# A selective-scan layer on one NeuronCore: when the next chunk's softplus, norm and gate projections are issued

## The chip, the cores and the metric

The kernel runs on one core of a Trainium2 chip. A core has five engines that run their own instruction queues in order and wait for each other through semaphores: TensorE (PE, matrix products into PSUM banks), VectorE (DVE), ScalarE (ACT, elementwise functions), GpSimd (POOL) and SyncE (SP, which issues most DMAs here). The metric is the device time of one execution in microseconds; the time before is the median of three runs.

## The reference, cut to what matters

The network has four layers; the change lies in the last one, a state-space layer, run here on an input of 3 images, 256 channels and 48 x 48 = 2304 tokens. `x` is the input of the layer after a group norm.

```python
mu = jnp.mean(xf, axis=-1, keepdims=True)
var = jnp.mean(jnp.square(xf - mu), axis=-1, keepdims=True)
xn = (xf - mu) * jax.lax.rsqrt(var + 1e-05) * norm_w + norm_b
xz = jnp.einsum('blc,dc->bld', xn, in_proj_w)
x_in, z = jnp.split(xz, 2, axis=-1)
...
xc = xc + conv_b[None, :, None]
u = jax.nn.silu(xc).transpose(0, 2, 1)
x_dbl = jnp.einsum('bld,ed->ble', u, x_proj_w)
...
dt = jax.nn.softplus(jnp.einsum('blr,dr->bld', dt_raw, dt_proj_w) + dt_proj_b)
A = -jnp.exp(A_log)

def step(hst, inp):
    dt_t, B_t, C_t, u_t = inp
    dA = jnp.exp(dt_t[:, :, None] * A)
    hst = hst * dA + dt_t[:, :, None] * B_t[:, None, :] * u_t[:, :, None]
    y_t = jnp.einsum('bdn,bn->bd', hst, C_t)
    return (hst, y_t)
...
y = ys.transpose(1, 0, 2) + u * D_param
y = y * jax.nn.silu(z)
out = jnp.einsum('bld,cd->blc', y, out_proj_w)
```

There are 512 inner channels and 16 states for each, so 8192 recurrences, each over 2304 tokens, for each of 3 images.

## The kernel before, in words

**Chunks and steps.** The layer runs over 18 chunks of 384 tokens (3 images, 6 chunks each). The scan of a chunk is eight steps (m = 0 to 3, one block of 128 inner channels each, times h = 0, 1, half of the states), and a step is eight scans over 384 tokens. A half step is four scans; the schedule counts half steps from 0 to 15 in a chunk, so half steps 8 to 11 are the fifth and sixth step, 12 to 15 the seventh and eighth. Below, "scan (11, 3)" is the last (counted from 0) of the four scans of half step 11.

**A scan and its decay.** Scan on DVE (L1785) takes a decay factor exp(dt A) that ACT has written to one of three PSUM slots (L1777). Right after issuing scan n the program issues decay n+3, which needs the slot that scan n frees. So the decay issued behind scan (j, p) is the one that scan (j, p+3) needs, three scans on (behind (13, 0) for (13, 3), behind (14, 0) for (14, 3)); ACT can be ahead of DVE by that much and no more. Between steps DVE also fills part of the next step's state tile (L1738; 2 instructions where the next step begins a block (h = 0), 1 where it does not) and, at the end of each h = 1 step, multiplies y with the gate (L1826). POOL fills the rest of the state tile (L1752) and, when all eight scans of a step are done, multiplies the states with C (L1802); PE then sums them (L1819).

**What runs beside the scan.** Everything else of the layer is prepared for later chunks while the scan of the current one runs: x norm two chunks ahead, projections, convolution taps, u, B, C, dt and the gate z one chunk ahead, the output projection one chunk behind. Lists (`plan`, `after`, `gating`, `last_of_all`) hand each stage a half step and a place in it: BEGIN, MID, DONE and LATE are behind the first, second, third and fourth scan and its decay, and PE_ is the end of the half step (behind the step's fills and its POOL product where the half step closes a step). Within one place, the order is that of the lists. `keep_order` holds PE, DVE, ACT and POOL to the order of issue, so a stage that waits for another engine holds up everything behind it on its own queue, the decays on ACT's among them.

**Two banks for all products.** All the preparing products use the same two PSUM banks, `bank[0]` and `bank[1]` (tiles `ps_g`). A product cannot start until the stage that reads the bank before it is done, and the ACT or DVE stage behind it cannot start until the product is.

**Stages on the path of the change** (names as in the code): `project_dt` (two products of 17 rows, L1317) gives dt for two of four blocks into both banks; `softplus` takes their absolute value (two ACT instructions, L1326), Exp of minus that (L1327) and Ln of one plus that (L1328); `take_dt` (four DVE instructions, L1333 and L1334) adds the positive part and makes dt times u; `keep_dt` (two ACT copies, L1338) empties the banks and sends dt and dt u to DRAM by two DMAs on SP. The second pair of blocks repeats all that. `group_scale` (two ACT, L1212), `less_mean` (four products, eight recorded instructions, L1221), `centre` (two copies, L1234, and a Square, L1236), `square_mean` (L1228), `inverse_root` (Ln and Exp on the bank, L1240 and L1241), `normalise` (one DVE product, L1245) and `tokens` (a short copy and two ACT, L1253 and L1255) are the norm. `project_z` and `take_z` (L1348, L1356) make z in four parts. `project_x`, `take_x`, `taps`, `take_u` (L1262, L1268, L1272, L1280) make u. The Silu of z and of u (L1285) sit between two loads of ACT's function tables.

## Time and profile before

| | us |
|---|---|
| median of 3 runs | 3430.42 (3429.17 to 3431.03) |
| profiled execution | 3427.89 |
| its span | 3426.0 |
| first scan of the layer starts at | 2019.0 |
| last scan starts at | 3403.1 |
| DVE, busy in the span | 2929.3 |
| ACT | 2379.0 |
| POOL | 1430.1 |

The scan layer is the last 1407 us of the span. A row of the profile's groups names the line, the engine, the operation, the output and inputs by tile, the count, the busy time with the mean of one, and the idle time of the engine just before these instructions with what ended it. The timeline gives start and length of each instruction or run of equal ones, in us from the start of the span, and in brackets the idle time before it and who ended it. Lengths are those that can be seen: a scan shows 0.93 us, and back to back they start every 0.85 us. The tables of stretches give the busy time of each engine in each stretch and the clock that TensorE was granted (PEclk, 1.00 is full speed).

### The profile page before, as it was taken

The page shows a single profiled execution, that of the slowest core. Times are in us where ns is not written, and L with a number is a line of the kernel's source. Part 1 is how long each engine was busy: PE and PEld are TensorE (multiplying, and loading weights), DVE is VectorE, ACT ScalarE, POOL GpSimd, SP SyncE. Part 2 cuts the span into 40 slices and gives each one's busy share as a digit, 9 for nine tenths or more (in the row PEclk, how much of TensorE's full clock was granted, in tenths as well). Part 3 has the DMA queues.
Part 4 walks back from the last instruction along what each step waited for, and adds up shares of the span by engine and source line. Part 5 has one row for each costly group of instructions (what it writes and reads, how often), then busy time and mean ns, then how long its engine had stood idle before and what let it go on. Part 6 is the DMA issues. An engine that isn't in the chain of part 4 may idle for free. (4 is left out here: it accounts for less than half of the span.)

```text
span 3426.0 us, 51520 instructions
## 1 busy us (share of the span) xinstructions
PE 3057.3 (89%) x19882; PEld 1446.1 (42%) x19882; DVE 2929.3 (86%) x3302; ACT 2379.0 (69%) x3596; POOL 1430.1 (42%) x385
## 2 busy tenths in 40 slices
PE   7999999999999999879999978788888888787885
PEld 4334343453333435447777743333333333333331
DVE  3799899959999896479965369999999999999997
ACT  2688888848888885432224458888788888888874
POOL 0000000000000000210000049999999999999997
PEclk9999999999999999989999998888898898888986
DMA  4000000010000002746501134545444444454441
GB/s 167 27 8 10 8 8 7 11 42 5 10 8 8 7 8 90 243 165 222 186 22 51 42 98 102 117 106 125 107 121 103 115 105 116 105 119 123 111 116 43
DMA packets 167170, 272.89 MB, mean 80 GB/s; under 512 B 30129, under 2 KB 134641, under 8 KB 164994
## 3 DMA queue, kind: packets, MB, share of 16 engines
q1 hardware_dynamic: 153682, 249.44, 26.8%
q10 hardware_dynamic: 13232, 20.06, 1.8%
q8 instruction: 158, 2.59, 0.3%
q14 instruction: 98, 0.80, 0.1%
HBM read 222.08 MB, written 47.10 MB: 79 GB/s over the span
## 5 line engine op out<-in xcount | busy, mean ns | idle before, releaser
L642 ACT ACTIVATE pt<-ps_s 128x1024 f32<-128x1024 f32 x972 | 942.3, 1022 | 154.8 <-PE ps_s L638 142.1
L1785 DVE TENSOR_TENSOR_SCAN hs<-ps_da,hs 128x385 f32<-128x385 f32 x1152 | 1005.4, 936 | 37.3 <-ACT ps_da L1777 34.3
L857 DVE TENSOR_TENSOR part<-part,pt 128x2048 f32<-128x2048 f32 x396 | 906.6, 2289 | 41.2 <-ACT pt L642 18.5
L1777 ACT ACTIVATE ps_da<-dtr,u 128x384 f32<-128x384 f32 x1152 | 657.6, 582 | 225.3 <-DVE hs L1785 214.3
L164 POOL TENSOR_TENSOR rstd<-ve,mhalf 128x2 f32<-128x2 f32 (+1 forms) x26 | 16.3, 629 | 1477.2 <-DVE ve L162 1477.2
L638 PE MATMUL ps_s<-q,kt 32*128 32x512 f32 (+1 forms) x4320 | 576.4, 592 | 0.1
L651 PE MATMUL acc<-pt,vt 128*32 128x512 f32 (+1 forms) x4320 | 520.9, 561 | 0.2
L1532 PE MATMUL ps_c<-vt,u 128*128 128x288 f32 x1728 | 431.3, 410 | 21.9 <-DVE u L263 21.9
L1802 POOL TENSOR_TENSOR hc<-hs,x 128x3072 f32<-128x3072 f32 x72 | 445.4, 6186 | 9.5 <-DVE hs L1785 7.5
L1802 POOL TENSOR_TENSOR hc<-hs,bc 128x3072 f32<-128x3072 f32 x71 | 437.7, 6165 | 8.0 <-DVE hs L1785 6.4
L1532 PEld LDWEIGHTS ps_c<-vt,u 128*128 128x128 f32 x1728 | 330.3, 192 | 118.0 <-issue 20.9
L638 PEld LDWEIGHTS ps_s<-q,kt 32*128 32x128 f32 x4320 | 195.3, 183 | 199.1 <-issue 120.2
L1819 PE MATMUL ps_y<-hc,u 128*32 128x384 f32 x2304 | 254.2, 566 | 18.9 <-POOL hc L1802 18.5
L1752 POOL TENSOR_TENSOR hs<-dtur,x 128x1536 f32<-128x1536 f32 x72 | 248.2, 3448 | 7.2 <-DMA dtur<-dtud 7.2
L1752 POOL TENSOR_TENSOR hs<-dtur,bc 128x1536 f32<-128x1536 f32 x72 | 248.8, 3456 | 0.0
L651 PEld LDWEIGHTS acc<-pt,vt 128*32 128x32 f32 x4320 | 94.4, 108 | 353.4 <-issue 326.7
L1272 PE MATMUL ps_g<-u 128*128 128x384 f32 x576 | 200.7, 497 | 21.5 <-ACT u L1268 21.4
L1317 PE MATMUL ps_g<-wconv,u 17*128 17x384 f32 x144 | 79.2, 684 | 105.2 <-ACT x L1338 79.6
L1272 PEld LDWEIGHTS ps_g<-u 128*128 128x128 f32 x576 | 107.5, 191 | 111.7 <-ACT u L1268 42.7
L1221 PE MATMUL ps_g<-wconv,u 128*128 128x384 f32 x144 | 85.7, 767 | 63.8 <-ACT x L1338 63.3
L1819 PEld LDWEIGHTS ps_y<-hc,u 128*32 128x32 f32 x2304 | 65.5, 119 | 180.7 <-issue 141.5
L322 POOL MEMSET xpad<- 128x212 f32 x12 | 5.7, 471 | 307.3 <-ACT xpad L1583 227.5
(249 smaller groups left out, 3825.1 us busy)
## 6 DMA issues: line engine op xcount, KB each, us to landing
wconv<-in_we SPq DMA_DIRECT2D x144, 384.0 KB, 4.2
dtr<-dtd SPq DMA_DIRECT2D x288, 192.0 KB, 3.7
dtur<-dtud SPq DMA_DIRECT2D x288, 96.0 KB, 4.1
wconv<-xd SPq DMA_DIRECT2D x36, 384.0 KB, 4.7
x<-bcd SPq DMA_DIRECT2D x72, 192.0 KB, 5.5
dtd<-x SPq DMA_DIRECT2D x36, 384.0 KB, 4.6
bc<-bcd SPq DMA_DIRECT2D x72, 192.0 KB, 5.0
yc<-ycat ACTq DMA_DIRECT2D x18, 576.0 KB, 4.7
```

Source lines behind the costliest of these rows:

```text
L638: nc.tensor.matmul(s[:, j, cols], kt[r, mt * P : (mt + 1) * P], q[r, :n], start=True, stop=True,)
L642: nc.scalar.activation(p[:, h0 : h0 + 2, :], s, AF.Exp)
L651: nc.tensor.matmul(acc[h * HD : (h + 1) * HD, :n], vt[:, mt, g * P + h * HD : g * P + (h + 1) * HD], p[:, h, cols], start=mt == 0, stop=mt ...
L857: ): nc.vector.tensor_tensor(part, first, p, ALU.add)
L1221: nc.tensor.matmul(bank[to], w3v["less"][:, int(to != ct), :], k.xg[:, ct, :], start=ct == 0, stop=ct == CT - 1,)
L1272: nc.tensor.matmul(bank[m % 2], w3v["taps"][:, m, tap, :], w3v["xi"][:, m % 3, tap : tap + CH], start=tap == 0, stop=tap == DCONV - 1,)
L1532: nc.tensor.matmul(pc[:, :HN], u[:, i, dy, ct, m * P : (m + 1) * P], vt[:, i, ct, dy * TW : dy * TW + HN], start=ct == 0 and dy == 0, stop ...
L1752: nc.gpsimd.tensor_tensor(states(s)[:, :, 2:4, 1:], chunks[at].rows[m][1].unsqueeze(1).broadcast_to([P, 2, 2, CH]), b_rows(s, 0, 2), ALU.mult,
L1777: nc.scalar.activation(slots[n % 3][:, 1 : CH + 1], chunks[at].rows[m][0][:, q, :], AF.Exp, scale=amat[:, col : col + 1],)
L1785: nc.vector.tensor_tensor_scan(b, slots[(8 * s + part) % 3][:, : CH + 1], b, 0.0, ALU.mult, ALU.add)
L1802: nc.gpsimd.tensor_tensor(hc, tiles[s][:, :, :, 1:], cb.broadcast_to([P, 2, 4, CH]), ALU.mult)
L1819: nc.tensor.matmul(k.y_ps[32 * q : 32 * q + 32, :CH], fold, hc[:, g, q, :], start=False, stop=h == 1 and g == 1,)
```

## The change

`softplus` becomes three stages (`take_abs`, `exp_of`, `log_of`), and the Square leaves `centre` for a stage of its own (`squares`). The plan's places move: softplus of the first pair goes from behind (9, LATE) to (9, MID), (9, DONE) and (9, LATE); its `take_dt` two places up, its `keep_dt` two, and `project_dt` of the second pair from the end of half step 10 to its second place. The second pair's softplus is taken apart over (10, LATE), (11, BEGIN) and (11, MID), with `take_dt` at (11, LATE) and `keep_dt` at (12, BEGIN). The norm moves up by two to four scans, from `group_scale` to `tokens`. The four parts of z are all made and taken within half steps 13 to 15, where before the last two were taken in half step 0 of the next chunk. `take_x` and `taps` of the third block move from (3, LATE) to (3, DONE). Each engine runs the same instructions as before, in another order. The code that runs ahead of the first scan calls the parts in the old order.

```diff
     def centre(k):
         for ct in range(CT):
             nc.scalar.copy(k.xg[:, ct, :], bank[ct])
+
+    def squares(k):
         k.sq = room(k, "sq")
         nc.scalar.activation(k.sq, k.xg, AF.Square)
...
-    def softplus(k, m0):
-
-        both = k.dt[:, m0 : m0 + 2, :]
+    def take_abs(k, m0):
         for j in range(2):
             nc.scalar.activation(k.dt[:, m0 + j, :], bank[j], AF.Abs)
+
+    def exp_of(k, m0):
+        both = k.dt[:, m0 : m0 + 2, :]
         nc.scalar.activation(both, both, AF.Exp, scale=-1.0)
+
+    def log_of(k, m0):
+        both = k.dt[:, m0 : m0 + 2, :]
         nc.scalar.activation(both, both, AF.Ln, bias=1.0)
...
     plan = [
-        (12, MID, 2, group_scale),
-        (12, PE_, 2, less_mean),
-        (13, LATE, 2, centre),
-        (13, PE_, 2, square_mean),
-        (14, MID, 2, inverse_root),
-        (15, MID, 2, normalise),
-        (15, LATE, 2, tokens),
...
-        (3, LATE, 1, lambda k: take_x(k, 2)),
-        (3, LATE, 1, lambda k: taps(k, 2)),
+        (3, DONE, 1, lambda k: take_x(k, 2)),
+        (3, DONE, 1, lambda k: taps(k, 2)),
...
-        (9, LATE, 1, lambda k: softplus(k, 0)),
-        (10, DONE, 1, lambda k: take_dt(k, 0)),
-        (10, LATE, 1, lambda k: keep_dt(k, 0)),
-        (10, PE_, 1, lambda k: project_dt(k, 2)),
-        (11, LATE, 1, lambda k: softplus(k, 2)),
-        (12, MID, 1, lambda k: take_dt(k, 2)),
-        (12, DONE, 1, lambda k: keep_dt(k, 2)),
+        (9, MID, 1, lambda k: take_abs(k, 0)),
+        (9, DONE, 1, lambda k: exp_of(k, 0)),
+        (9, LATE, 1, lambda k: log_of(k, 0)),
+        (10, BEGIN, 1, lambda k: take_dt(k, 0)),
+        (10, MID, 1, lambda k: keep_dt(k, 0)),
+        (10, MID, 1, lambda k: project_dt(k, 2)),
+        (10, LATE, 1, lambda k: take_abs(k, 2)),
+        (11, BEGIN, 1, lambda k: exp_of(k, 2)),
+        (11, MID, 1, lambda k: log_of(k, 2)),
+        (11, LATE, 1, lambda k: take_dt(k, 2)),
+        (12, BEGIN, 1, lambda k: keep_dt(k, 2)),
+        (11, DONE, 2, group_scale),
+        (12, BEGIN, 2, less_mean),
+        (12, LATE, 2, centre),
+        (13, BEGIN, 2, squares),
+        (13, BEGIN, 2, square_mean),
+        (13, LATE, 2, inverse_root),
+        (14, MID, 2, normalise),
+        (14, LATE, 2, tokens),
     ]
 
     after = [
-        (0, MID, 0, lambda k: k.at and take_z(k, 2, 0)),
-        (0, MID, 0, lambda k: k.at and take_z(k, 3, 1)),
...
     gating = [
-        (13, PE_, 1, lambda k: project_z(k, 0, 0)),
-        (14, DONE, 1, lambda k: take_z(k, 0, 0)),
-        (14, PE_, 1, lambda k: project_z(k, 1, 0)),
-        (15, MID, 1, lambda k: take_z(k, 1, 0)),
-        (15, PE_, 1, lambda k: project_z(k, 2, 0)),
-        (15, PE_, 1, lambda k: project_z(k, 3, 1)),
+        (13, BEGIN, 1, lambda k: project_z(k, 0, 0)),
+        (13, PE_, 1, lambda k: project_z(k, 1, 0)),
+        (13, LATE, 1, lambda k: take_z(k, 0, 0)),
+        (14, DONE, 1, lambda k: take_z(k, 1, 0)),
+        (14, DONE, 1, lambda k: project_z(k, 2, 0)),
+        (14, PE_, 1, lambda k: project_z(k, 3, 1)),
+        (15, MID, 1, lambda k: take_z(k, 2, 0)),
+        (15, DONE, 1, lambda k: take_z(k, 3, 1)),
     ]
```

More of the change, by code (lines that the diff above doesn't have):

```diff
@@ L1458, in early_preparation @@
         centre(k)
+        squares(k)
         tap_matrices(0)
@@ L1491, in early_preparation @@
             stage(k)
+            if stage is centre:
+                squares(k)
             yield
@@ L1506, in early_preparation @@
             yield
-            softplus(k, m)
+            take_abs(k, m)
+            exp_of(k, m)
+            log_of(k, m)
             yield
```

## The prediction

> **What bounds the kernel now.** I read the page's groups first, to see which engine is full in the scan layer; then the list of waits from 2000 us on; then, for one chunk, the timelines of DVE, PE, ACT and SP and the clock by stretches.

> ```profile
> L1785 DVE TENSOR_TENSOR_SCAN hs<-ps_da,hs 128x385 f32<-128x385 f32 x1152 | 1005.4, 936 | 37.3 <-ACT ps_da L1777 34.3
> L1802 POOL TENSOR_TENSOR hc<-hs,x 128x3072 f32<-128x3072 f32 x72 | 445.4, 6186 | 9.5 <-DVE hs L1785 7.5
> L1752 POOL TENSOR_TENSOR hs<-dtur,x 128x1536 f32<-128x1536 f32 x72 | 248.2, 3448 | 7.2 <-DMA dtur<-dtud 7.2
> ...
> PE ps_g L1317 <- ACT x L1338: 79.6, 17, 5.6
> PE ps_g L1221 <- ACT x L1338: 63.3, 16, 4.4
> ```

> DVE runs through: its scans waited 37.3 us in all, 34.3 of them for a decay that ACT had not written. In DVE's timeline over all chunks these waits sit in three places: scan (4, 3), 0.73 us in each of 17 chunks (12.2 us); scan (14, 3), 0.65 to 0.91 in 10 chunks (7.8); scan (15, 1), about 0.8 in 16 chunks (12.7). Together 32.7 us. Chunks 1 to 15 take 76.7 to 77.9 us (mean 77.4), some 75.4 without waits. POOL is nearly as full: in its timeline a fill and a product follow each other every 9.53 us, eight times a chunk, 76.25 us, and it waited for DVE 28 times. So what the change can win is at most 77.4 - 76.25 = 1.1 us a chunk, 19 us in 17, even if every wait went.

> ```profile
> 2477.31 1.81 DVE L1785 TENSOR_TENSOR_SCAN hs<-ps_da,hs 128x385 f32<-128x385 f32 x2 [0.80 <-ACT ps_da L1777]
> 2480.04 0.96 DVE L1785 TENSOR_TENSOR_SCAN hs<-ps_da,hs 128x385 f32<-128x385 f32 x1 [0.92 <-ACT ps_da L1777]
> ...
> 2449.34 1.55 PE L1317 MATMUL ps_g<-wconv,u 17*128 17x384 f32 x4 [1.47 <-ACT wconv L1299]
> ...
> 2458.85 2.92 PE L1317 MATMUL ps_g<-wconv,u 17*128 17x384 f32 x4 [4.68 <-ACT x L1338]
> ...
> 2469.93 5.49 PE L1221 MATMUL ps_g<-wconv,u 128*128 128x384 f32 x8 [4.04 <-ACT x L1338]
> 2476.86 1.56 PE L1228 MATMUL ps_g<-wconv,mean 128*128 128x384 f32 x4 [1.44 <-ACT wconv L1236]
> ...
> 2489.34 2.87 PE L1262 MATMUL ps_g<-u 128*128 128x387 f32 x8 [0.38 <-ACT x L1356]
> ...
> 2474.17 0.48 ACT L1234 COPY wconv<-ps_g 128x384 f32<-128x384 f32 x1 [0.45 <-PE ps_g L1221]
> 2475.45 0.48 ACT L1234 COPY wconv<-ps_g 128x384 f32<-128x384 f32 x1 [0.80 <-PE ps_g L1221]
> ...
> 2453.00:2462.00 9.00, 4.32 (x9) 1.48 (x8) 8.93 (x14) 6.82 (x14) 9.00 (x3) 0.50 0.45 100
> 2470.00:2476.00 6.00, 5.42 (x8) 2.42 (x8) 6.00 (x8) 4.11 (x10) 5.77 (x2) 0.51 1.01 248
> 2476.00:2482.00 6.00, 5.14 (x29) 2.25 (x29) 4.28 (x6) 5.29 (x11) 6.00 (x2) 1.00 0.03 12
> 2486.00:2498.00 12.00, 11.09 (x45) 5.36 (x43) 12.00 (x15) 8.80 (x20) 11.73 (x3) 1.00 0.37 97
> ```

> What to see: PE has much idle time in half steps 9 to 13, and there its granted clock (third number from the end of a stretch) is half. The same four records of `project_dt` take 1.55 us at full clock and 2.92 at half. `less_mean` takes 5.49 (4.38 and 5.26 in other chunks, where the clock comes up on the way), and `centre` on ACT waits for it although it has four scans' time; the two waits of DVE follow from that.

> **The change, step by step.** No instruction is added. What changes is the time between a product and its reader, and the decays queued behind the reader on ACT. I walk the chunk shown, with these lengths from its rows: scan and decay every 0.85 and 0.51 us, a decay readable 0.59 after its start, copy or Abs every 0.37, Exp and Ln 0.84 each (each waits for the one before), `take_dt` 2.11, gate 0.45, fills 0.86 or 2.53.

> *(a) `take_dt` at (10, BEGIN).* `project_dt` is unmoved: banks ready at 2450.25 and 2450.90. ACT: decay 2449.79, Abs 2450.30 and 2450.95, decay 2451.32, Exp 2451.83, decay 2452.59, Ln 2453.10, done 2453.94. DVE is at `take_dt` one scan into half step 10, at 2453.01. It waits 0.95, with the scans behind it. Before, it came two scans later and Ln was hidden by them. Low end 0.95; 2.3 if that product too is at half clock (2.92 for 1.55).

> *(b) scan (11, 3).* `take_dt` ends at 2456.08, scan (10, 1) follows, `keep_dt` copies at 2457.55, and `project_dt` of the second pair starts 0.52 behind the first copy (as 2458.33 to 2458.85): 2458.07. PE has then been idle for 3.9 us, and the row next to it (4.68 idle) was at half clock: banks at 2459.71 and 2460.99. ACT stands in Abs until 2461.4, so the decay for scan (11, 3) is there at 2461.99, wanted at 2461.18: 0.83. At full clock 0.

> *(c) `take_dt` at (11, LATE).* The decay and a small copy, Exp at 2462.01, a decay, Ln 2463.28 to 2464.12; DVE, behind scan and gate, is there at 2463.31: 0.84. With (b) at full clock 0.32.

> *(d) scan (13, 3).* `keep_dt` copies come at 2470.28, behind scan (12, 0), `less_mean` starts at 2470.80. At half clock `centre` gets its banks 4.24 and 5.52 later (2469.93 to 2474.17 and 2475.45): 2475.04 and 2476.32, and the decay behind the copies is there at 2477.3. Scan (13, 3) wants it at 2474.78: 2.5. `centre` now has three scans for what took four and more. With the other chunks' 5.26 and 4.38 it is 2.3 and 1.4; at full clock (2.87, the eight records of L1262) 0. I take 2.0, near the mean of the three rows.

> *(e) what follows.* Square ends at 2478.15, `square_mean` starts. At full clock (1.56, then 1.45 for `project_z`) `normalise` waits 0.2 for Exp, and scan (15, 3) some 0.2, as ACT now holds `tokens` and two `take_z` that wait for PE: 0.4. At half clock 1.35 more for each product: `normalise` 1.5, scan (14, 3) 1.1 behind `take_z`, together 3.0. Before, the clock was up by then, and 1.44 us of pause followed; now it is 1.9 with less work behind. I take 1.5, between the ends.

> *(f) half steps 0 to 4.* Moving `take_z` out of (0, MID) frees both banks early. `project_x` started 2.88 us into the chunk after `take_z` and ran almost up to `taps` (0.53 idle). Now it can start at about 0.1 and ends at 2.9, while `taps` still waits for `take_x` at (1, MID), 6.3: 3.4 us of idle that was not there. Where that halves the clock for one stretch, the 5.43 us of `taps` grow by 1.7, and PE is behind by that at `project_x` of the third block, where ACT already waited 0.34 us for it ahead of the Silu of z. The place of `take_x` ahead of the decay of (3, 3), not behind it, costs the Silu another 0.4. The waits at scans (3, 3) and (4, 3) are then 0.73 + 0.4 + 1.7 = 2.8 to 2.95; at full clock 1.1. I take 2.4.

> Waits that go: (14, 3) and (15, 1) in their old form, and 0.73 at (4, 3), all contained in the 32.7. DMAs: `keep_dt` issues two each time, and SP's queue is why that gains and costs nothing: the eight loads of B and C (L1309) were being issued from 2457.52 for 5.30 us, and dt's store stood behind them. The rows of dt are read by the decay behind (15, 1), some 5 us after they land. If that cover went, the decay would wait for a transfer; the walk only lengthens the time. POOL's queue is not touched; with DVE slower it waits more. PE's sums of states stand behind `project_z`, a fraction of the 9.5 us until their gate.

> Sum: (a, b, c, f) 0.95 + 0.83 + 0.84 + 2.4 = 5.02 in 17 chunks, 85.3; (d, e) 3.5 in 16 chunks, 56.0; less 32.7: +108.6. On the profiled execution's 3427.9 us that is 3536.5. The median of the runs was 2.5 above that execution: **3539**.

> [...] The clock row is 0.50 from 2453 on, though PE had only paused 0.62 and 1.47 us and then worked on small products. [...] I go by the row.

> **The rivals.** *A. The clock holds.* All at full clock: (a) 0.95, (c) 0.32, (f) 1.1 in 17 chunks, (e) 0.4 in 16: 46.7 - 32.7 = +14, 3444. For: clock 1.00 in the stretch from 2486. Against: 0.50 in 2453 to 2462, where the change adds no work to PE. *B. Faster: the waits go and POOL bounds.* The split leaves ACT no more than 1.4 us between two decays where it was 2.6 in one piece, and the norm gets off the end of the chunk. If new waits stay under 0.9 us a chunk, POOL's 76.25 decides: 3430.4 - 19 = 3411. Against: (a) alone is 0.95, and its product is at full clock already. *C. No change:* old and new waits balance near 1.9 us a chunk, 3424 to 3437; (a) and (f) at their least already make 2.05.

> **How the numbers follow.** Forecast (slower, 3480 to 3580) 0.82; A and what lies below 3480 0.11; C 0.04; B 0.03. The range: 3480 is (d) 0, (e) 0.4 and (f) half way down; 3580 is (a) half clocked and (e) 0.75 more, 23 + 12, with (d) at 2.5. All terms at their ends would give 3444 and about 3605. About 0.2% is what a measurement of this kernel can tell from no change: faster 0.03, same 0.04, slower 0.93.

> **What would show it.** After: waits of DVE for ACT between 100 and 160 us in place of 34; waits at `take_dt` (L1333) for Ln, 0 now; `less_mean`'s reader waiting 2 us and more; POOL idle by some 7 us a chunk; clock 0.50 in half steps 10 to 13 and, for (f), also in half steps 1 and 2. I am wrong if PE shows full clock there, if Ln is done when DVE comes, or if a chunk takes less than 80 us.

## The result, and the profile after

The changed kernel takes 3533.1 us (median of 4 runs, 3529.3 to 3536.4), the kernel before 3429.8 (3427.3 to 3431.0): 1.0303 times as long, 95% interval 1.029 to 1.0315. The forecast of 3539 us, slower, holds, and the range holds the time. The medians are 103.3 us apart. The profiled execution, the longest of the four, has a span of 3534.6 us, 108.6 more than before, and a mean granted clock of 0.919 (before 0.936).

In the code after the change the line numbers are: scan 1801, decay 1793, fill 1754, POOL's product 1818, `take_dt` 1339 and 1340, Ln of dt 1334, `keep_dt` 1344, `project_dt` 1319, `project_x` 1264, `taps` 1274, `less_mean` 1221, `square_mean` 1228, `normalise` 1247. From the page's groups (the last two lines are the kernel before, for POOL's second product and for the taps):

```profile
L1801 DVE TENSOR_TENSOR_SCAN hs<-ps_da,hs 128x385 f32<-128x385 f32 x1152 | 1009.3, 938 | 100.7 <-ACT ps_da L1793 97.5
L1818 POOL TENSOR_TENSOR hc<-hs,x 128x3072 f32<-128x3072 f32 x72 | 445.5, 6188 | 62.2 <-DVE hs L1801 59.5
L1818 POOL TENSOR_TENSOR hc<-hs,bc 128x3072 f32<-128x3072 f32 x71 | 438.0, 6169 | 63.9 <-DVE hs L1801 63.2
L1274 PE MATMUL ps_g<-u 128*128 128x384 f32 x576 | 225.5, 545 | 66.6 <-ACT u L1270 66.6
L1319 PE MATMUL ps_g<-wconv,u 17*128 17x384 f32 x144 | 81.1, 699 | 85.0 <-ACT x L1344 59.3
...
L1802 POOL TENSOR_TENSOR hc<-hs,bc 128x3072 f32<-128x3072 f32 x71 | 437.7, 6165 | 8.0 <-DVE hs L1785 6.4
L1272 PE MATMUL ps_g<-u 128*128 128x384 f32 x576 | 200.7, 497 | 21.5 <-ACT u L1268 21.4
```

The scans wait 100.7 us in place of 37.3. POOL, which had been idle for 17.5 us ahead of the products of these two rows (13.9 of them for the scans), is now idle for 126.1 (122.7 for the scans): it no longer bounds anything. The taps, untouched by the diff but for the place of one block, cost 225.5 us in place of 200.7. The list of waits of DVE from 2020 us on (us in all, times, the longest) shows who ends them:

```profile
DVE hs L1801 <- ACT ps_da L1793: 97.5, 86, 2.6
DVE ps_g L1339 <- ACT x L1334: 29.3, 34, 1.6
DVE wconv L1247 <- ACT ps_g L1243: 5.8, 8, 1.2
```

97.5 + 29.3 + 5.8 = 132.6 us for ACT, where there were 34.3. The second row is the wait of `take_dt` for Ln, twice a chunk, which was not there. One chunk of it in DVE's timeline (start, length; idle time before it in brackets):

```profile
2490.14 0.57 DVE L1339 SCALAR_TENSOR_TENSOR ps_g<-ps_g,x 128x384 f32<-128x384 f32 x1 [0.83 <-ACT x L1334]
...
2498.27 0.96 DVE L1801 TENSOR_TENSOR_SCAN hs<-ps_da,hs 128x385 f32<-128x385 f32 x1 [0.79 <-ACT ps_da L1793]
2500.37 0.57 DVE L1339 SCALAR_TENSOR_TENSOR ps_g<-ps_g,x 128x384 f32<-128x384 f32 x1 [0.69 <-ACT x L1334]
...
2513.34 0.96 DVE L1801 TENSOR_TENSOR_SCAN hs<-ps_da,hs 128x385 f32<-128x385 f32 x1 [2.26 <-ACT ps_da L1793]
2517.26 0.95 DVE L1247 TENSOR_TENSOR wconv<-wconv,ps_g 128x768 f32<-128x768 f32 x1 [0.40 <-ACT ps_g L1243]
2519.72 0.96 DVE L1801 TENSOR_TENSOR_SCAN hs<-ps_da,hs 128x385 f32<-128x385 f32 x1 [0.64 <-ACT ps_da L1793]
```

In order these are the steps (a), (b), (c), (d) and two of (e) of the prediction, the last one at scan (14, 3). PE and ACT behind them, in their timelines (the first line is the taps in the kernel before):

```profile
2492.74 5.43 PE L1272 MATMUL ps_g<-u 128*128 128x384 f32 x16 [0.53 <-ACT u L1268]
...
2447.72 8.44 PE L1274 MATMUL ps_g<-u 128*128 128x384 f32 x16 [2.94 <-ACT u L1270]
...
2485.56 1.55 PE L1319 MATMUL ps_g<-wconv,u 17*128 17x384 f32 x4 [1.47 <-ACT wconv L1301]
2494.31 2.92 PE L1319 MATMUL ps_g<-wconv,u 17*128 17x384 f32 x4 [3.76 <-ACT x L1344]
2507.13 5.18 PE L1221 MATMUL ps_g<-wconv,u 128*128 128x384 f32 x8 [3.02 <-ACT x L1344]
```

```profile
2511.37 0.48 ACT L1234 COPY wconv<-ps_g 128x384 f32<-128x384 f32 x1 [2.22 <-PE ps_g L1221]
2512.34 0.48 ACT L1234 COPY wconv<-ps_g 128x384 f32<-128x384 f32 x1 [0.49 <-PE ps_g L1221]
2512.72 0.59 ACT L1793 ACTIVATE ps_da<-dtr,u 128x384 f32<-128x384 f32 x1
```

The stretches with taps and with half steps 9 to 12 (busy time of the engines; the granted clock is the third number from the end):

```profile
2447.50:2456.00 8.50, 8.28 (x16) 4.45 (x16) 7.76 (x9) 4.35 (x9) 8.23 (x3) 0.63 0.01 2
2488.00:2512.00 24.00, 14.72 (x42) 5.30 (x34) 20.63 (x27) 14.09 (x28) 20.48 (x5) 0.50 0.71 164
```

`less_mean` runs 5.18 us, at half clock for nearly all of it (0.54 from 2507.13 to 2512.31), ACT stands before its two copies until 2512.34, and the decay that scan (13, 3) needs is issued behind them, at 2512.72, as the prediction walked it. The taps show 8.44 us for 5.43; the clock is at half for most of that stretch too (0.63 over all of it).

### The profile page after: what moved, and what is told of

It reads as the page before. It is cut to its first block, busy times and chain, and to the rows that moved or that the text cites. A ratio compares the mean times of both kernels' runs of the same rounds, so it can differ in the third digit from the quotient of the medians.

```text
span 3534.6 us, 51514 instructions
## 1 busy us (share of the span) xinstructions
PE 3107.3 (88%) x19882; PEld 1462.8 (41%) x19882; DVE 2939.5 (83%) x3302; ACT 2369.1 (67%) x3596; POOL 1431.2 (40%) x385
## 3 DMA queue, kind: packets, MB, share of 16 engines
q1 hardware_dynamic: 153682, 249.44, 26.3%
## 5 line engine op out<-in xcount | busy, mean ns | idle before, releaser
L1801 DVE TENSOR_TENSOR_SCAN hs<-ps_da,hs 128x385 f32<-128x385 f32 x1152 | 1009.3, 938 | 100.7 <-ACT ps_da L1793 97.5
L1274 PE MATMUL ps_g<-u 128*128 128x384 f32 x576 | 225.5, 545 | 66.6 <-ACT u L1270 66.6
L1835 PE MATMUL ps_y<-hc,u 128*32 128x384 f32 x2304 | 260.8, 579 | 21.7 <-POOL hc L1818 21.3
L1274 PEld LDWEIGHTS ps_g<-u 128*128 128x128 f32 x576 | 119.2, 212 | 171.1 <-ACT u L1270 89.0
L1354 PE MATMUL ps_g<-u 128*128 128x384 f32 x288 | 122.6, 564 | 15.1 <-ACT sz L1362 7.5
```

Source lines behind the costliest of these rows:

```text
L1274: nc.tensor.matmul(bank[m % 2], w3v["taps"][:, m, tap, :], w3v["xi"][:, m % 3, tap : tap + CH], start=tap == 0, stop=tap == DCONV - 1,)
L1354: nc.tensor.matmul(bank[j], w("in", ct * 512 + m * P, P), k.xn[:, ct, DCONV - 1 :], start=ct == 0, stop=ct == CT - 1,)
L1801: nc.vector.tensor_tensor_scan(b, slots[(8 * s + part) % 3][:, : CH + 1], b, 0.0, ALU.mult, ALU.add)
L1835: nc.tensor.matmul(k.y_ps[32 * q : 32 * q + 32, :CH], fold, hc[:, g, q, :], start=False, stop=h == 1 and g == 1,)
```

## The experiments

Each was timed against the kernel before on the same chip; ratios are to it. Diffs are against the changed kernel unless the text says otherwise. "Waits" are idle times of DVE in the trace of the run.

**Undoing parts.** First only the dt part of the change; norm, gate and `take_x` at their old places:

```diff
+        (12, MID, 2, group_scale),
+        (12, PE_, 2, less_mean),
...
+        (3, LATE, 1, lambda k: take_x(k, 2)),
...
-        (11, DONE, 2, group_scale),
-        (12, BEGIN, 2, less_mean),
...
-        (13, BEGIN, 1, lambda k: project_z(k, 0, 0)),
+        (13, PE_, 1, lambda k: project_z(k, 0, 0)),
```

> Only the softplus in three parts with its take_dt, keep_dt and second project_dt stays moved; norm, z and the third take_x are at their old places. Theory (three separate costs, each a product that is too close to its reader): the waits (a), (b), (c) at take_dt (10), scan (11,3) and take_dt (11) stay, 1.04 + 0.79 + 0.69 = 2.5 us in 17 chunks, and the old 32.7 us at (4,3), (14,3), (15,1) come back: 3430 + 43 + 4 = 3477 us. Rival (the norm and z moves carry the loss, the softplus parts are free or gain): 3430 or less.

Measured: 3472.2 us, ratio 1.0128 (1.0111 to 1.0145). Waits: `take_dt` (10, BEGIN) 17.3 us, scan (11, 3) 13.4, `take_dt` (11, LATE) 11.7: 42.4 from the dt part, the same as in the whole change to 0.3 us, and the total is near the 3477 expected. A wait of 0.28 at scan (13, 1) is new (4.4 us), and the old ones at (14, 3) and (15, 1) shrink from 20.5 to 11.8. The dt part does cost by itself, whatever the norm does.

Second, the last two parts of z taken in half step 0 again:

```diff
+        (0, MID, 0, lambda k: k.at and take_z(k, 2, 0)),
+        (0, MID, 0, lambda k: k.at and take_z(k, 3, 1)),
...
-        (15, MID, 1, lambda k: take_z(k, 2, 0)),
-        (15, DONE, 1, lambda k: take_z(k, 3, 1)),
```

> The changed kernel with the last two parts of z taken in half step 0 again, so that project_x has to wait for its banks as before. Theory (PE pauses for 3.4 us before taps and its clock halves): the pause is gone, taps run at full clock, waits at (3,3) and (4,3) fall from 44.8 us to some 1.1 us in each of 17 chunks, 19 us: 3533 - 27 = 3506. Rival (take_x ahead of the decay at half step 3 makes that wait): 3533, waits there unchanged.

Measured: 3520.8 us, 1.0272 (1.0255 to 1.0289): 12 us gained of 27 expected. The waits at scans (3, 3) and (4, 3) went from 44.8 to 26.3 us, but those from (13, 3) on rose from 45.5 to 51.8. The taps are as short as before the change (mean 497 ns), but the pause has only moved ahead of `project_x`, in its groups row (same columns as above):

```profile
L1274 PE MATMUL ps_g<-u 128*128 128x384 f32 x576 | 200.7, 497 | 23.6 <-ACT u L1270 23.6
L1264 PE MATMUL ps_g<-u 128*128 128x387 f32 x288 | 112.8, 537 | 39.0 <-ACT x L1362 19.6 <-ACT sz L1362 19.5
```

With z made early in half steps 13 to 15, taking it late leaves PE 39 us idle there, and `project_x` meets the half clock (mean 537 ns, 500 in the changed kernel). So the theory's place was right and its gain too high.

Third, `take_x` and `taps` of the third block at (3, LATE) again:

```diff
-        (3, DONE, 1, lambda k: take_x(k, 2)),
-        (3, DONE, 1, lambda k: taps(k, 2)),
+        (3, LATE, 1, lambda k: take_x(k, 2)),
+        (3, LATE, 1, lambda k: taps(k, 2)),
```

> The changed kernel with take_x and taps of the third block at (3, LATE) again. Theory: only the 0.4 us go that the Silu starts later, 17 times: 3533 - 7 = 3526, the clock is still half in half steps 1 and 2 of most chunks. Rival (its place makes the waits at (3,3) and (4,3)): they fall to 0.73 in each chunk, 12 us in all: 3533 - 32 = 3501.

Measured: 3513.4 us, 1.0244 (1.0227 to 1.0261), between the two. Scans (3, 3) and (4, 3) wait 19.2 us in place of 44.8, and `normalise` and the scans behind it 6 more. Scan (4, 3) waits 0.72 in most chunks, 0.49 less than the 1.21 that it shows in most chunks of the next run, where the taps are at full clock in every chunk but the first: that is the part of the place, 8 us in 17 chunks. The other 17 of the 25.6 us come from the clock: in chunks 1 to 15 the taps took over 5.5 us 4 times, in the changed kernel 11 times, with the same pause ahead of them. Why the clock is at half behind the same pause in some chunks only is not shown; what the traces have on it is in the last section.

**Adding work to PE.** If the half clock is at fault, more PE work should make the kernel faster. Dummy products whose result nobody reads, 8 of them behind `project_x`:

```diff
+    def warm(n):
+        for _ in range(n):
+            nc.tensor.matmul(
+                whole[0][:, 392:512], ident, ident[:, :120], start=True, stop=True
+            )
...
         (0, PE_, 1, lambda k: project_x(k, 1)),
+        (0, PE_, 1, lambda k: warm(8)),
```

> The changed kernel with 8 products of the identity by 120 of its columns, read by nobody, issued on PE behind project_x in half step 0: more work, nothing moved. Theory (the clock): the pause before taps is filled, PE keeps full clock in half steps 0 to 4, waits at (3,3) and (4,3) fall to 1.1 us a chunk: 3533 - 27 = 3506. Rival (the banks or the queue order, not the clock): no gain, or later by the added work, 3533 to 3550.

Measured: 3508.7 us, 1.0236 (1.0218 to 1.0254). 24 us gained by 33 us of added PE work. The taps took 5.43 us in every chunk but the first, scan (3, 3) waits in the first chunk alone, and (4, 3) waits 1.0 to 1.2 in each: 21.7 us in place of 44.8. Further on nothing was gained in sum: scan (13, 3) waits 38.2 us in place of 28.3, and `normalise` and the scans behind it about as much less.

The same for half steps 8 to 13, in the changed kernel without and with the 8, and in the kernel before:

```diff
         (8, BEGIN, 1, project_u),
+        (8, BEGIN, 1, lambda k: warm(4)),
...
                 spread_pe(chunks[steps[s + 2][0]], steps[s + 2][1])
+                if m == 2 and at < last:
+                    warm(18)
```

> The changed kernel with dummy products (128x120, result unused) in PE's pauses of half steps 8 to 13: 4 behind project_u, 18 behind the ones that spread dt u in half step 9, 14 behind the second project_dt, 15 behind the state sums of half step 11, 4 behind less_mean. PE only gets more work; no place of the change is undone. Theory (the half clock is what makes the banks late): scan (11, 3) loses its wait (13.4 us), take_dt at (11, LATE) keeps 0.32 of 0.69 (6.3 less), scan (13, 3) loses its wait (28.3), and normalise and the scans behind it keep 0.4 a chunk of 17.2 us (10.8 less): 58.8 us, and some 57 stops of DVE fewer at 0.085 us each, 4.8: about 3470. take_dt at (10, BEGIN) keeps its wait for Ln, and half steps 1 to 4 theirs. Rival (the new places themselves are too early for ACT's queue, at any clock): 3520 to 3545.

> The changed kernel with the dummy products of both earlier ones: those in half steps 8 to 13 and the 8 behind project_x. Theory (rival A of the prediction, the clock holds): the 3470 expected with the first set less the 24 us that the second set gave by itself: about 3446, near the 3444 of rival A; what is left is take_dt's wait for Ln, 17 us, and 1.2 us a chunk at scan (4, 3). [...]

> The kernel before, nothing moved, with dummy products in PE's pauses of half steps 8 to 13 (4 behind project_u, 22 in half step 9, 4 behind the second project_dt, 22 behind the state sums of half step 11, 4 behind less_mean). Theory (its waits at scans (14, 3) and (15, 1), 20.5 us together, are the half clock as well): both go, (4, 3) stays, and POOL's 76.25 us a chunk bounds: 3408 to 3414, faster than both kernels. Rival (they are set by the order of ACT's queue, or POOL holds the rest up): 3424 to 3432.

All three missed by far: 3691.3 (1.0772, 1.0754 to 1.079), 3669.4 (1.0698, 1.068 to 1.0715) and 3624.4 us (1.0572, 1.0555 to 1.059). The list of waits of the first names the cause:

```profile
DVE ps_g L1345 <- PE ps_g L1271: 82.7, 16, 6.5
```

The dummies (L1271) wrote unused columns of bank 0, and `take_dt` (L1345 there), which uses other columns of that bank, waits for them: the program's own dependencies put them in order. ACT's Abs waits for them in the same way, 118.3 us in that run, and the scan that stands behind it, (11, 3), waits 116.5 us in place of 13.4. These runs say nothing of the clock. The dummies were therefore moved to unused columns of `ps_r`, a tile that nobody reads in those pauses:

```diff
-                whole[0][:, 392:512], ident, ident[:, :120], start=True, stop=True
+                spare["t"][:, 0, 392:512], ident, ident[:, :120], start=True, stop=True
```

> As the first try with dummies in half steps 8 to 13 of the changed kernel, but the dummy products write to unused columns of ps_r, which nobody reads in those pauses, so that take_dt no longer waits for them: 4 behind project_u, 18 behind spread_pe in half step 9, 12 behind the second project_dt, 14 behind the state sums of half step 11, 4 behind less_mean. Theory (the half clock makes the banks late): no wait at scan (11, 3) (13.4 us less), 0.3 a chunk at take_dt (11, LATE) (6 less), none at scan (13, 3) (28 less), 0.4 a chunk from normalise on (11 less), and some 5 for the overlap that a stop of DVE loses: about 3470; if one of the products stays at half clock, 3470 to 3500. Rival (the new places are too early at any clock): 3520 to 3545.

> The kernel before, nothing moved, with dummy products in unused columns of ps_r in PE's pauses of half steps 8 to 13 (4 behind project_u, 22 behind spread_pe in half step 9, 3 behind the second project_dt, 22 behind the state sums of half step 11, 6 behind less_mean). Theory (its waits at scans (14, 3) and (15, 1), 20.5 us, are the half clock as well): both go and POOL's 76.25 us a chunk bounds: 3408 to 3414, faster than both kernels. Rival (they are set by the order of ACT's queue, or POOL takes their place): 3424 to 3432.

Measured: 3500.4 us, 1.0211 (1.0194 to 1.0228), at the upper end of the theory, and 3440.0, 1.0037 (1.0023 to 1.0051), above both sides. In the changed kernel scan (11, 3) waits 3.7 us in place of 13.4, `take_dt` (11, LATE) 7.6 in place of 11.7, and everything from `normalise` on nothing in place of 17.2. Scan (13, 3) still waits 26.4, although `less_mean` runs at full clock in every chunk (2.75 us): it now stands behind the dummies themselves and starts 1 to 3 us late. In the kernel before, the waits at (14, 3) and (15, 1) are gone, though DVE also comes there later, since its fills, which read `ps_r`, now wait 39.0 us for the dummies. So the counts were refitted; in the kernel before the last 4 went to bank 0 behind `centre`:

> The changed kernel with the dummy products refitted so that DVE and less_mean no longer wait for them: in ps_r 6 behind project_u, 20 behind spread_pe in half step 9, 12 behind the second project_dt, 7 behind the state sums of half step 11, 4 behind less_mean, and the 8 in bank 0 behind project_x. Theory (rival A of the prediction: the clock holds): waits of DVE left are 0.93 at take_dt (10, BEGIN) and 0.23 at (11, LATE) as with the first free-bank try, 1.21 at scan (4, 3), none at (11, 3), under 0.3 at (13, 3) and behind: 2.4 to 2.7 a chunk, where the kernel before has 1.9: 3432 to 3448. Rival (the places are too early at full clock too, scan (13, 3) waits 1 us or more): 3455 or more.

> The kernel before, nothing moved, with the dummy products refitted so that DVE's fills no longer wait for them: in ps_r 6 behind project_u, 22 behind spread_pe in half step 9, 14 behind the state sums of half step 11, and 4 in bank 0 behind centre. In the try before, the waits at scans (14, 3) and (15, 1) were gone and two waits for the dummies themselves (22.1 and 17.4 us) were there instead. Theory: without these 39.5 the 3440 become 3402, and POOL's 76.25 us a chunk stops it at 3408 to 3416, faster than before. Rival (POOL or ACT's queue takes the place of what goes): 3424 to 3432.

Measured: the changed kernel 3451.9 us, 1.0068 (1.0055 to 1.0082), between its two sides; the kernel before with dummies 3411.5, as its theory had it, **0.9946 (0.9932 to 0.9959), faster than both kernels**. Groups of the latter, and in the last two lines of the kernel before without dummies:

```profile
L1801 DVE TENSOR_TENSOR_SCAN hs<-ps_da,hs 128x385 f32<-128x385 f32 x1152 | 1004.5, 936 | 25.7 <-ACT ps_da L1793 22.6
L1818 POOL TENSOR_TENSOR hc<-hs,x 128x3072 f32<-128x3072 f32 x72 | 446.5, 6202 | 3.0 <-DVE hs L1801 2.0
L1818 POOL TENSOR_TENSOR hc<-hs,bc 128x3072 f32<-128x3072 f32 x71 | 438.9, 6181 | 2.3 <-DVE hs L1801 1.2
...
L1221 PE MATMUL ps_g<-wconv,u 128*128 128x384 f32 x144 | 59.6, 565 | 21.3 <-ACT x L1338 20.8 <-ACT wconv L1212 0.5
L1317 PE MATMUL ps_g<-wconv,u 17*128 17x384 f32 x144 | 55.9, 507 | 11.5 <-ACT x L1338 7.8 <-ACT wconv L1299 3.4
...
L1221 PE MATMUL ps_g<-wconv,u 128*128 128x384 f32 x144 | 85.7, 767 | 63.8 <-ACT x L1338 63.3
L1317 PE MATMUL ps_g<-wconv,u 17*128 17x384 f32 x144 | 79.2, 684 | 105.2 <-ACT x L1338 79.6
```

Means of 565 and 507 ns for `less_mean` and `project_dt` (767 and 684 in the kernel before) go with a granted clock of 0.95 from 2010 to 3400 us (0.87 in the kernel before). POOL waits 5.3 us in these rows, and 11 of chunks 1 to 15 take 76.3 to 76.4 us: POOL's 76.25 is the bound, as the prediction read it. The wait at scan (14, 3) is gone; at (15, 1) 8.5 of 12.7 us stay, 0.40 in the chunks with a full clock, and in a chunk that POOL bounds they cost nothing.

In the changed kernel `project_dt` has the same 507 ns; no wait is left at (11, 3), 3.9 us at `take_dt` (11, LATE), none from `normalise` on. Scan (13, 3) waits over 1 us in 11 of 16 chunks and not at all in five. Two chunks of PE's timeline, one of each kind:

```profile
2555.01 2.73 PE L1389 MATMUL ps_r<-ident 128*128 128x120 f32 x14 [2.64 <-DVE hs L1772]
2557.52 3.55 PE L1221 MATMUL ps_g<-wconv,u 128*128 128x384 f32 x8
...
2713.47 1.82 PE L1389 MATMUL ps_r<-ident 128*128 128x120 f32 x14 [2.64 <-DVE hs L1772]
2715.42 2.85 PE L1221 MATMUL ps_g<-wconv,u 128*128 128x384 f32 x8
```

The dummies wait 2.64 us for a fill that reads `ps_r`. In 11 chunks the clock falls behind that pause (in the first pair's, 0.86 from 2550 to 2562 us): the dummies then take up to 3.34 us for 1.82 and hold `less_mean` back, and scan (13, 3) waits (first pair). In seven of these 11, `less_mean` itself is back at full clock (2.75 to 2.88 us) and only starts some 1.2 us late, so there the wait is the dummies'. In the other five chunks the clock holds (in the second pair's, 1.00 from 2708 to 2720 us), `less_mean` starts right behind the copy that frees its bank, as it does without dummies, takes 2.85 us, and there is no wait (second pair). These five take 77.94 to 78.00 us: 0.6 more than the mean of 77.4 before, and 1.55 more than the 76.42 that most chunks of the kernel before take with its clock held up. That difference is what the new places cost by themselves at full clock, 26 us in 17 chunks, and 3411.5 + 26 is some 3438 us, an estimate.

**What keeps the clock up.** Last, the 8 dummies behind `project_x` of 17 rows, not 128:

```diff
-                whole[0][:, 392:512], ident, ident[:, :120], start=True, stop=True
+                whole[0][:, 392:512], ident[:17], ident[:17, :120], start=True, stop=True
```

> The changed kernel with the same 8 dummy products behind project_x as in the run that gave 3509 us, in the same place and of the same number of columns, but of 17 rows in place of 128, as project_dt's products have. Theory (the clock goes by how many of the array's rows work, as project_dt's products, busy for 1.55 us, did not hold it in any trace here): the taps are at half clock again in most chunks, scans (3, 3) and (4, 3) wait 40 us or more together: 3520 to 3540. Rival (it goes by PE's busy time alone): taps at full clock, these waits 22 us: 3506 to 3512.

Measured: 3528.3 us, 1.0295 (1.0278 to 1.0312). PE's timeline in one chunk with 128 rows, and one with 17:

```profile
2522.59 1.94 PE L1271 MATMUL ps_g<-ident 128*128 128x120 f32 x16
2525.83 5.43 PE L1280 MATMUL ps_g<-u 128*128 128x384 f32 x16 [1.30 <-ACT u L1276]
```

```profile
2524.77 2.04 PE L1271 MATMUL ps_g<-ident 17*128 17x120 f32 x16
2527.87 7.12 PE L1280 MATMUL ps_g<-u 128*128 128x384 f32 x16 [1.06 <-ACT u L1276]
```

Both sets keep PE busy for 2 us and leave a pause of 1.1 to 1.3. Of the taps of chunks 1 to 15, none was slowed with 128 rows, 7 with 17 rows and 11 without dummies; scans (3, 3) and (4, 3) wait 21.7, 33.1 and 44.8 us. The 128-row set also kept the taps at 5.43 us in all these chunks of the two other runs of the changed kernel that have it (3669.4 and 3451.9 us), 45 of 45 in all, so that is no accident of where the chunks fall. The time is the theory's, but the waits lie between the two (40 or more were expected). Whether the small products do a little for the clock is not shown: without these dummies 4 to 15 of the 15 were slowed in the other runs of the changed kernel with `project_x` early (4 with `take_x` late, 15 in the run of 3500.4 us), and 7 lies among these.

## Why the prediction was right

Its terms against the changed kernel's trace, sums over all chunks:

| step | predicted | measured | each |
|---|---|---|---|
| (a) `take_dt` (10, BEGIN) waits for Ln | 16.2 | 17.6 | 1.04 |
| (b) scan (11, 3) | 14.1 | 13.4 | 0.79 |
| (c) `take_dt` (11, LATE) waits for Ln | 14.3 | 11.7 | 0.69 |
| (d) scan (13, 3) behind `centre` | 32.0 | 28.3 | 1.77 |
| (e) `normalise`, scans (14, 3), (15, 3) | 24.0 | 17.2 | 1.08 |
| (f) scans (3, 3), (4, 3) | 40.8 | 44.8 | 2.64 |
| old waits that go | -32.7 | -32.7 | |
| sum | 108.6 | 100.3 | |
| DVE busier | none | 10.2 | |

All six waits are where the walk put them, and each product named as cold (at half clock) was, the taps and `square_mean` in part of the chunks. One named as being at full clock was not always: the first `project_dt` took 1.6 to 2.3 us for 1.55 in 6 of 17 chunks, which is in (a). The sum of the waits is 8 us high, above all by (e), where the clock came up in time for `square_mean` in more chunks than assumed (it took under 1.7 us in 8 of 16). The 1.7 us by which (f) has the taps grow was an estimate: in chunks 1 to 15 they took 5.43 us four times, 7.12 six times and 8.34 to 8.44 five times. A term of 10 us was missing: DVE's busy time grew from 2929.3 to 2939.5 with the same instructions. A scan back to back starts every 0.85 us, but the one behind a wait shows 0.96 before the next can go on. The steps hold 132 stops where the old waits were 43: 89 more, at 0.11 us each 9.8. (With the dt part alone, 61 stops more go with 6.7 us more, 0.11 each as well.) In the table (f) holds 1.6 us at scan (3, 3) of the first chunk that were there before too; by the lists of waits the growth is 132.6 - 34.3 = 98.3, and with 10.2 that is 108.5 of the 108.6. The two errors nearly cancel: that the predicted sum is the very growth of the span is luck, the more so as that execution is the longest of four.

That the half clock makes the waits (b), (c) in part, (d), (e) and the larger part of (f) was argued from rows only; the dummy products show it. With them (b) and (e) vanish and (f) falls to 1.2 a chunk; (d) vanishes in the five chunks where `less_mean` started in time and ran at full clock. (a) stays, as walked: 0.94 a chunk in the run of 3500.4 us and 0.97 in that of 3451.9, where its product is at full clock. It is the order of ACT's queue, and the first experiment shows that it comes with the dt part alone.

Rival A (the clock holds, 3444) was right as a what-if: with the clock held up the same code would take some 3438 us, the estimate above from the chunks in which it is. Rival B's bound (3411) is real too, but the change doesn't lead there: the kernel before reaches 3411.5 with its clock held up. The wait at (14, 3) was for the cold `less_mean` and not for the place of softplus or norm: in the kernel before it comes in the ten chunks where `less_mean` takes 5.23 us or more and in none of the six where it takes 4.54 or less, and it goes with the dummies. A part of that at (15, 1) goes with them too. Moving the stages closer together shortened the time that had covered a cold product.

The prediction went by the clock's rows, and the trace after has the same: the clock was at 0.50 from 2488 on though the pause just before, in the timeline above, was 1.47 us, and `less_mean` behind 3.02 us of pause was cold (5.18 us, where it takes 2.85 in the five chunks of the run of 3451.9 us where the clock holds).

## What to carry to other kernels

Before moving a stage closer to its product, read the product's length in every chunk beside the granted clock: slack that looks idle may be covering a half-clocked product. Where such a product ends the waits, work added to PE's pause can be worth more than a new order: here 0.5% faster against 3% slower. Here such filler needed a PSUM bank that nobody else touched in that time, and a count that ended before the next product was due; else it became the wait.

## What the runs showed of the hardware

```profile
2448.52:2451.93 3.41, 2.58 (x20) 1.08 (x20) 3.41 (x5) 2.95 (x7) 3.41 (x2) 1.00 0.25 77
2451.93:2455.34 3.41, 2.24 (x12) 0.50 (x4) 3.38 (x6) 3.35 (x7) 3.41 (x2) 0.50 0.00 0
2086.70:2090.11 3.41, 1.97 (x7) 0.95 (x6) 3.41 (x5) 3.07 (x7) 3.41 (x1) 1.00 0.55 185
2090.11:2093.52 3.41, 3.41 (x24) 1.32 (x25) 2.60 (x4) 2.81 (x7) 3.41 (x2) 1.00 0.02 5
```

In the first PE is busy for 2.58 us, 76% of the stretch, and the clock behind it is 0.50; in the second for 1.97 us, 58%, and the clock stays at 1.00. PE's busy time alone does not sort such stretches: of those at full clock in the scan layer of the kernel before, half clock followed shares of up to 0.76, and full clock stayed behind shares from 0.52 up. The first stretch is for the larger part the 17-row products of `project_dt`, the second the norm's products of 128 rows. The 17-row run fits that in kind: behind 2.04 us of 17-row dummies the taps were slowed in 7 of 15 chunks, behind 1.94 us of 128-row dummies in none. That rows are what counts is an inference from these traces, and row counts between 32 and 128 do not occur in these layers.

Which chunks are cold follows a pattern in the kernel before: from the third chunk on `less_mean` takes about 5.5, 4.4 and 5.2 us in turn, and the wait at (14, 3) came in ten of 16 chunks. A chunk of 77.4 us is 22.67 times the 3.413 us, and three chunks are 68.0 times. That a chunk's place against the changes of the clock decides whether it is cold is the author's estimate from these numbers; no run shows it by itself. What a few us of a change of this kind owe to that place is not told apart by these runs.
